# Loading the later image pairs as 32x32 blocks and turning them on VectorE instead of TensorE

## Chip, cores and metric

One NeuronCore of a Trainium2 chip. The metric is device time in microseconds (us) of one execution, the median of several runs. All data is 32-bit float.

## The reference

`x` has 32 images of 14 x 14 tokens with 512 channels. Two layers, each with a group norm (32 groups of 16 channels, over a whole image) in front and a residual around it:

```python
x = x + _L0_conv_ref(_gn(x), block_w, block_b, fc1_w, fc1_b, fc2_w, fc2_b, gammas)
x = x + _L1_conv_ref(_gn(x), W)

# layer 0: 18 blocks, one after the other
for i in range(18):
    nx = gelu(einsum('bhwc,cd->bhwd', x, block_w[i]) + block_b[i])
    if i in (11, 14, 17):
        gates = softmax over 3 anchors of fc2(gelu(fc1(mean of nx over the tokens)))
        nx = nx + gamma[t] * sum of gates * anchors
    x = nx
    if i in (1, 4, 9): anchors.append(x)

# layer 1: a 3x3 convolution, 'SAME', 32 groups of 16 channels
```

## The kernel before, in words

**Tiles.** Activations lie with channels on the 128 partitions and tokens along the row. A tile of work `t` holds two images (N = 392 tokens), a pair `p` two tiles (four images); there are 8 pairs, 0 to 7. The 512 channels are four chunks `c` of 128, two to a "quarter" tile of 128 x 784 (`quarter`, L84).

**A step** is one block (of 18) for one pair: 144 steps. It is done as seven half-size matrix products (a Strassen form; `block`, L371), each of 8 TensorE records (`product`, L387, the matmul is L390). Their PSUM accumulators are X, Y and Z. ScalarE copies them out (`save`, L423), VectorE adds (`add`, L427: c from X, Y or Z), ScalarE applies gelu (L403, or L410 where the token mean is needed), VectorE makes the differences for the next step (`pre_adds`, L369). X is accumulated three times in one bank: after the third product a copy of it is taken, after the fifth an `add` reads it, and the seventh product adds to it again.

**Order of the work.** Everything else is placed between products by hand. A step has seven ticks, one after each product; `calendar` holds what is emitted in a tick, and `put` (L124) looks for the first tick whose budget (`ROOM`, L111; us of VectorE and ScalarE per tick) has room for the cost that the caller names. Each engine works in order, and so does SyncE (SP), which issues nearly all DMAs: a DMA that waits holds up those behind it. The order of steps interleaves two pairs: q's first steps stand among p's last, then q goes on alone with its blocks 6 to 11, and so on.

**The weights** of a step are loaded by `load_block` (L328) in tick 0 of the step before. The four weight sums s0 to s3 of a block are computed once, for pair 0, and kept in DRAM (`skeep`); later pairs load them (`sums`, L346) in ticks 2 to 5 of the step before, each into the one buffer that its product has just set free.

**A pair's start** (`plan_start`, L295): t0 is the first tick of its first step, LEAD is 35 ticks. For each tile, four pieces of 98 tokens x 512 channels are loaded by SP (`load_in`, L245; tag "xin", three buffers), three of them in tick t0 - LEAD - 6, and turned (`turn_in`, L248): four TensorE transposes (L258, tile `tpi`), two copies by ScalarE (L263) that also change the token order within an image from row-major to column-major. The turned tile is written to DRAM (`xkeep`, L271), as the residual needs it at the end. Then the norm's statistics (`stats_in`, L196), scales, and the norm itself in place (L284). Pair 0 is loaded and turned before the first step by the same two functions.

**A pair's end.** After block 17, `gate_base` (L570) on VectorE starts the routed sum, POOL issues four DMAs that add `xkeep` to it in place (`residual`, L666), and `gate_part` (L580), `gate_last` (L594) and `gate_add` (L602) finish it. Layer 1 follows in batches of two pairs: statistics, columns written to DRAM (`x2d`, L699, in pieces of 224 B), reloaded (L817), the convolution as matmuls with band matrices (L838), a sum (L848), a turn back (L862) and the store. The steps between block 17 of pair p and the first step of pair p + 2 are the six steps of pair p + 1 with blocks 6 to 11; so the tick t0 - LEAD - 8 of a pair p + 2 is the last tick of block 17 of pair p.

Of the kernel before, what the change touches and what calls it, by code (L numbers as in the profile page):

```python
# [9 lines left out]
F32 = mybir.dt.float32  # L10
# [9 lines left out]
def kernel(  # L20
# [20 lines left out]
    nc = tc.nc  # L41
    P = 128
    B, H, W, C = x.shape
    HW = H * W
    NCK = C // P
    NH = NCK // 2
    NI = 2
    N = NI * HW
    NT = B // NI
    NPAIR = NT // 2  # L50
    NB4 = 2 * NI
    TS = 4
# [3 lines left out]
    NTG, _, HID = fc1_w.shape  # L56
# [14 lines left out]
    fpool = ctx.enter_context(tc.tile_pool(name="fpool", bufs=1))  # L71
    qpool = ctx.enter_context(tc.tile_pool(name="qpool", bufs=38))
    tmp = ctx.enter_context(tc.tile_pool(name="tmp", bufs=6))
    inpool = ctx.enter_context(tc.tile_pool(name="inpool", bufs=3))
    outpool = ctx.enter_context(tc.tile_pool(name="outpool", bufs=2))
    cvpool = ctx.enter_context(tc.tile_pool(name="cvpool", bufs=2))
    small = ctx.enter_context(tc.tile_pool(name="small", bufs=2))
# [6 lines left out]
    def quarter(name):  # L84
        return qpool.tile([P, NH, N], F32, tag="q", name=name)
# [8 lines left out]
    for p in range(NPAIR - 1):  # L94
        q = p + 1
        if q < NPAIR - 1:
            parts = [(q, 0, 3), (p, 12, 15), (q, 3, 6), (p, 15, 18), (q, 6, 12)]
        else:
            parts = [
                (q, 0, 6), (p, 12, 15), (q, 6, 12), (p, 15, 17), (q, 12, 15), (p, 17, 18),  # L100
                (q, GAP, 0), (q, 15, 18),
            ]
# [12 lines left out]
    def at(tick, fn, *args):  # L115
        calendar[tick].append((fn, args))

    def room(e, tick):
        return left[e].get(tick, ROOM[e][tick % NP7] if tick < tend else TAIL[e])
# [4 lines left out]
    def put(first, need, fn, *args):  # L124

        tick = first
        while any(room(e, tick) < us for e, us in need.items()):
            tick += 1
        for e, us in need.items():
            left[e][tick] = room(e, tick) - us  # L130
        at(tick, fn, *args)
        return tick
# [53 lines left out]
    def stats_tiles(name):  # L186
        d = {"name": name}
        for v, shape in (
            ("st", [NR, 6]), ("mr", [3, NR]), ("dv", [NR, 2]), ("ve", [NR]), ("y", [NR]), ("e", [NR]),
        ):  # L190
            d[v] = small.tile([P] + shape, F32, tag=v, name=f"{v}_{name}")
        return d
# [15 lines left out]
    def scales_mean(d, lo=0, hi=NR):  # L208
        st, mean, dv = d["st"][:, lo:hi], d["mr"][:, 0, lo:hi], d["dv"][:, lo:hi]
        ps = group_sums(f"mps_{d['name']}_{lo}", st[:, :, 1::3], hi - lo)  # L210
        nc.vector.tensor_scalar(mean, ps, 0.5, None, ALU.mult)
        nc.vector.tensor_tensor(
            dv, st[:, :, 1::3], mean.unsqueeze(2).to_broadcast([P, hi - lo, 2]), ALU.subtract
        )
        nc.vector.tensor_mul(dv, dv, dv)
        nc.vector.scalar_tensor_tensor(dv, dv, HW / 2.0, st[:, :, 2::3], ALU.mult, ALU.add)

    def scales_rstd(d, lo=0, hi=NR):

        ps = group_sums(f"vps_{d['name']}_{lo}", d["dv"][:, lo:hi], hi - lo)  # L220
        ve = d["ve"][:, lo:hi]
        nc.vector.tensor_scalar(ve, ps, 1.0 / HW, 1e-5, ALU.mult, ALU.add)
        nc.gpsimd.tensor_tensor(d["y"][:, lo:hi], ve, mhalf[:, lo:hi], ALU.pow)

    def scales_newton(d, lo=0, hi=NR):
        ve, y, e, mr = d["ve"][:, lo:hi], d["y"][:, lo:hi], d["e"][:, lo:hi], d["mr"]
        nc.vector.tensor_mul(e, y, y)
        nc.vector.tensor_mul(e, e, ve)
        nc.vector.tensor_scalar(e, e, -0.5, 1.5, ALU.mult, ALU.add)
        nc.vector.tensor_mul(mr[:, 1, lo:hi], y, e)  # L230
        nc.vector.scalar_tensor_tensor(
            mr[:, 2, lo:hi], mr[:, 0, lo:hi], -1.0, mr[:, 1, lo:hi], ALU.mult, ALU.mult
        )


    xkeep = [
        tc.dram_tile([2, P, NH * N], F32, name=f"xkeep{t}") for t in range(NT)
    ]
    starts = {}
    pst = {}  # L240
# [54 lines left out]
    def plan_start(p):  # L295

        t0 = NP7 * at_step[p, 0]
        parts = [(2 * p + n, s) for n in range(2) for s in range(TS)]
        NIN = 3
        a = t0 - LEAD  # L300
        turned = []
        for j, (t, s) in enumerate(parts):
            at(t0 - LEAD - 6 if j < NIN else turned[j - NIN], load_in, t, s)
            turned.append(put(max(a, turned[j - NIN] + 4 if j >= NIN else 0), {"act": 0.6}, turn_in, t, s))
            a = turned[j] + 1
        b = 0
        for n in range(2):
            for c in range(NCK):
                b = max(b, put(
                    turned[n * TS + TS - 1] + 1, {"dve": 1.0}, stats_in, 2 * p + n, c  # L310
                ))
        b = put(b + 1, {"dve": 0.8}, lambda: scales_mean(pst[p]))
        b = put(b + 1, {"dve": 0.2}, lambda: scales_rstd(pst[p]))
        b = put(b + 2, {"dve": 0.8}, lambda: scales_newton(pst[p]))
        e = b
        for c in range(NCK):
            e = max(e, put(b, {"dve": 1.6}, norm_in, p, c))
        b = e

        assert b < t0  # L320
        at(t0 - 1, take_start, p)
# [290 lines left out]
    def plan_head(p, i):  # L612

        k = at_step[p, i]
        t1 = NP7 * (k + 1)
        name = f"{p}_{i}"
        ti = TARGETS.index(i)
        box = boxes[p, i] = {}
        end = k == len(steps) - 1
        if p == 0:  # L620
            at(t1 + 1, gate_differences, k, ti)
        at(t1 + (0 if end else 1), gate_hidden, k, ti, name, box)
        box["base"] = {
            (h, n): put(t1, {"dve": 1.0}, gate_base, p, i, h, n) for h in range(2) for n in range(2)
        }
        a = t1 + (1 if end else 2)
        while room("dve", a) < 2.2:
            a += 1
        at(a, gate_logits, k, name, box)
        return put(a, {"dve": 2.2}, gate_softmax, ti, name, box)  # L630

    def plan_gates(p, t, a, chunks):

        box = boxes[p, t]
        last = max(a, *box["base"].values())
        for cs in chunks:
            for n in range(2):
                b = a + 1
                adds = []
                for c in cs:  # L640
                    b = put(b, {"act": 0.75}, gate_last, p, t, box, cs, c, n)
                    for i in range(NI):
                        last = max(last, put(a, {"dve": 0.43}, gate_part, p, box, c, n, i))
                    adds.append((c, b + 1))
                for c, b in adds:
                    last = max(last, put(b, {"dve": 0.5}, gate_add, box, cs, c, n))
        return last
# [312 lines left out]
    LEAD = 35  # L960
    for k in range(len(steps)):
        p, i = steps[k]
# [26 lines left out]
    for p in range(NPAIR):  # L989
        plan_differences(p)  # L990
        for i in TARGETS[:-1]:
            a = plan_gates(p, i, plan_head(p, i), [[0, 1], [2, 3]])
# [5 lines left out]
    for p in range(1, NPAIR):  # L998
        plan_start(p)
    ended = {p: plan_end(p) for p in [*range(NPAIR - 2), NPAIR - 1, NPAIR - 2]}  # L1000
    b = NP7
    for g in range(C // CG):
# [3 lines left out]
        for dx in range(3):  # L1006
            b = put(b, {"dve": 1.15 if dx else 0.6}, build_band, g, dx)
# [39 lines left out]
```

## Time and profile before

| what | value |
|---|---|
| median of 3 runs | 2988.8 us (2988.3 to 2991.35) |
| the profiled execution: its time / its span | 2990.1 us / 2988.3 us |
| granted TensorE clock | 0.994 |
| busy: PE / DVE / ACT / POOL | 99% / 58% / 49% / 3% |
| turn, PE records: L258 | 256 matmuls (64 turns of four transposes), 34.4 us busy |
| turn, ScalarE: L263 | 128 copies, 35.4 us busy |
| DMA queue of SP (q1) | 355,178 packets, 436.85 MB, 46.4% of the 16 engines' span |
| DMA queue of ACT (q10) | 25,792 packets, 13.65 MB, 1.7% |
| DMA queue of POOL (q0) | 4,608 packets, 12.85 MB, 2.5% |
| loads of x by SP | 60 of 196 KB, median issue 412 ns |

How to read it: PE is TensorE's matmuls, PEld its weight loads, DVE is VectorE, ACT ScalarE, POOL GpSimd, SP SyncE. A group line names the line of code, the engine, the operation, output and input tiles and shape, and how often it came; then busy us in total, mean ns of one, and how long its engine sat idle just before, with what ended that. The chain of work that ended last is followed back from the last instruction. A timeline row has start, length, engine, line, operation and count, with the idle time before it in brackets. Packets are the pieces in which DMA engines move data.

### The profile page before, as it was taken

To read this page: it belongs to the slowest core of one execution; us is meant where nothing else is said; L and a number is where in the kernel's file an instruction comes from. 1 tells how busy PE (TensorE), PEld (TensorE's weight loads), DVE (VectorE), ACT (ScalarE), POOL (GpSimd) and SP (SyncE) were. 2 spreads that over 40 slices of the span, in tenths; PEclk is the share of its full clock that TensorE was granted. 3 is DMA by queue.
4 is the path that set the end of the run, shared out by engine and by line. 5 is a ranking of instruction groups with operands and counts; after the bars stand their busy time and mean duration, and the time that the engine had idled before them with its cause. 6 is when DMAs were issued, how large, how long until landed. Compare 5 with 4: busy or idle time off the path is not lost.

```text
span 2988.3 us, 31804 instructions
## 1 busy us (share of the span) xinstructions
PE 2945.5 (99%) x10113; PEld 1812.9 (61%) x10113; DVE 1734.0 (58%) x3309; ACT 1457.6 (49%) x3467; POOL 77.8 (3%) x60
## 2 busy tenths in 40 slices
PE   8999999999999999999999999999999999999986
PEld 5555555555566566666666666666666665656666
DVE  6877786655467454673546635565455653545663
ACT  4445445545455444554545544445445554544551
POOL 0000000000000000000000000000000000000010
PEclk9999999999999999999999999999999999999997
DMA  4444436633365345553455544555445653343678
GB/s 159 154 165 139 162 125 191 178 115 116 126 195 156 129 142 162 185 159 132 146 164 174 173 133 133 173 166 173 139 132 168 173 161 121 124 135 118 206 220 210
DMA packets 385743, 465.36 MB, mean 156 GB/s; under 512 B 150715, under 2 KB 213290, under 8 KB 385578
## 3 DMA queue, kind: packets, MB, share of 16 engines
q1 hardware_dynamic: 355178, 436.85, 46.4%
q0 software_dynamic: 4608, 12.85, 2.5%
q10 hardware_dynamic: 25792, 13.65, 1.7%
q8 instruction: 81, 1.33, 0.2%
q14 instruction: 84, 0.69, 0.1%
HBM read 381.48 MB, written 81.79 MB: 155 GB/s over the span
## 4 chain that ended last, share of the span: by engine, by line
PE 98%; DMA 1%; DVE 1%; issue 0%; ACT 0%; SPq 0%; DVEq 0%
PE x L390 51%; PE z L390 25%; PE y L390 13%; PE cps L838 5%; PE lps L522 1%; PE tpo L862 1%; PE tpi L258 1%; PE hps L506 1%; DMA tw<-in_L_conv_W_dram 0%; DMA w<-in_L_conv_fc_w_dram 0%; PE warm L950 0%; DMA w<-in_L_conv_block_w_dram 0%; DMA x2d<-xc 0%; PE mps_b L203 0%; DMA x<-x2d 0%
## 5 line engine op out<-in xcount | busy, mean ns | idle before, releaser
L390 PE MATMUL x<-t,s 128*128 128x392 f32 x2304 | 810.0, 494 | 0.0
L403 ACT ACTIVATE o<-c,bias 128x392 f32<-128x392 f32 x720 | 440.7, 620 | 663.0 <-DVE c L427 658.3
L390 PEld LDWEIGHTS x<-t,s 128*128 128x128 f32 x2304 | 432.5, 190 | 297.5
L427 DVE TENSOR_TENSOR c<-x,c 128x392 f32<-128x392 f32 x288 | 160.8, 565 | 515.5 <-PE x L390 423.8
L423 ACT COPY c<-x 128x392 f32<-128x392 f32 x576 | 278.4, 483 | 352.6 <-PE x L390 347.7
L390 PE MATMUL x<-t,w 128*128 128x392 f32 x1152 | 403.1, 493 | 0.9 <-DVE c L427 0.9
L390 PE MATMUL z<-t,s 128*128 128x392 f32 x1152 | 403.1, 493 | 0.0
L390 PE MATMUL z<-o,s 128*128 128x392 f32 x1088 | 380.9, 493 | 0.0
L390 PE MATMUL y<-o,w 128*128 128x392 f32 x1088 | 380.5, 492 | 0.0
L390 PE MATMUL x<-o,w 128*128 128x392 f32 x1088 | 380.3, 492 | 0.0
L427 DVE TENSOR_TENSOR c<-y,c 128x392 f32<-128x392 f32 x288 | 162.9, 566 | 294.3 <-PE y L390 206.7
L390 PEld LDWEIGHTS x<-t,w 128*128 128x128 f32 x1152 | 217.8, 190 | 157.9 <-DVE c L427 1.5
L390 PEld LDWEIGHTS z<-t,s 128*128 128x128 f32 x1152 | 217.0, 190 | 152.2
L369 DVE TENSOR_TENSOR t<-o,o 128x784 f32<-128x784 f32 x272 | 264.1, 971 | 65.4 <-ACT o L403 63.5
L390 PEld LDWEIGHTS x<-o,w 128*128 128x128 f32 x1088 | 206.4, 190 | 147.2
L390 PEld LDWEIGHTS y<-o,w 128*128 128x128 f32 x1088 | 205.1, 190 | 145.6
L390 PEld LDWEIGHTS z<-o,s 128*128 128x128 f32 x1088 | 205.0, 190 | 145.3
L369 DVE TENSOR_TENSOR t<-o,t 128x784 f32<-128x784 f32 x272 | 264.2, 971 | 4.7
L423 ACT COPY c<-z 128x392 f32<-128x392 f32 x288 | 139.2, 483 | 206.3 <-PE z L390 206.2
L427 DVE TENSOR_TENSOR c<-z,c 128x392 f32<-128x392 f32 x288 | 159.1, 563 | 118.8 <-PE z L390 118.0
L410 ACT ACTIVATE o<-c,bias 128x196 f32<-128x196 f32 x288 | 129.4, 450 | 91.0 <-DVE c L427 90.2
L403 ACT ACTIVATE o<-x,bias 128x392 f32<-128x392 f32 x240 | 137.5, 582 | 72.8 <-PE x L390 67.0
(107 smaller groups left out, 2061.2 us busy)
## 6 DMA issues: line engine op xcount, KB each, us to landing
w<-in_L_conv_block_w_dram SPq DMA_DIRECT2D x144, 1024.0 KB
s<-skeep SPq DMA_DIRECT2D x504, 256.0 KB
x2d<-xc SPq DMA_DIRECT2D x128, 224.0 KB
x<-x2d SPq DMA_DIRECT2D x64, 448.0 KB
skeep<-s SPq DMA_DIRECT2D x72, 256.0 KB
bw<-band SPq DMA_DIRECT2D x38, 384.0 KB
xkeep<-xt SPq DMA_DIRECT2D x32, 392.0 KB
o<-xkeep POOLq DMA_DIRECT2D x32, 392.0 KB, 7.6
```

Source lines behind the costliest of these rows:

```text
L258: nc.tensor.transpose(tp[:, c * TP : (c + 1) * TP], xs[:, c * P : (c + 1) * P], ident[:TP, :TP])
L369: nc.vector.tensor_tensor(t[j], i0, i1, ALU.subtract)
L390: nc.tensor.matmul(acc[d][:, :N], lhsT=lhsT[:, kk, d * P : (d + 1) * P], rhs=rhs[:, kk, :], start=first and kk == 0, stop=kk == NH - 1, sk ...
L403: nc.scalar.activation(o[:, d, :], srcs[d], AF.Gelu_apprx_tanh, bias=bias[:, r : r + 1])
L410: nc.scalar.activation(o[:, d, sl], srcs[d][:, sl], AF.Gelu_apprx_tanh, bias=bias[:, r : r + 1], accum_out=pooled[:, c, m : m + 1],)
L423: nc.scalar.copy(cs[d], acc[d][:, :N])
L427: nc.vector.tensor_tensor(cs[d], acc[d][:, :N], cs[d], ALU.add)
L506: nc.tensor.matmul(hps[:, :NB4], lhsT=w1[:, kk, :], rhs=box["pooled"][:, kk, :], start=(kk == 0), stop=(kk == NCK - 1),)
L522: nc.tensor.matmul(lps[:, m * NB4 : (m + 1) * NB4], lhsT=w2[:, m * P : (m + 1) * P], rhs=h, start=True, stop=True,)
L838: nc.tensor.matmul(pv[:, :, lo:hi], lhsT=d["bw"][:, g, dy], rhs=xv[:, :, lo + dy - 1 : hi + dy - 1], start=j == 0, stop=j == 2, skip_group ...
L862: nc.tensor.transpose(tp[:NV, j * P : (j + 1) * P], d["xs"][:, g, 0, v * NV : (v + 1) * NV], ident)
```

## The change

Only pairs 1 to 7 are touched. (1) `copy_in` copies the four images of a pair from x to a DRAM tensor `xcol[p]` whose tokens stand in column-major order within an image, 30 ticks before t0 - LEAD. (2) `load_blocks` loads one chunk of 128 channels of one tile as blocks: partition q*32+j holds, for channel group q of 32 and token j of each block of 32 tokens, 32 channels; that is 12 blocks of 32 tokens, in pieces of 32 channels (128 B), by four DMAs. Since 392 is not a multiple of 32, the last 32 tokens of all four chunks are loaded once more for each tile (`xr`, four DMAs). (3) `turn_blocks` turns the blocks with one VectorE transpose of 128 x 384, and with every second chunk one of 128 x 64 for the last tokens. (4) The plan charges VectorE instead of ScalarE for a turn, loads the first four chunks in tick t0 - LEAD - 8, lets several turns stand in one tick, and puts a chunk's statistics after its half tile. The pool of loaded pieces has four buffers instead of three. `stats_in`, the norm, `xkeep` and all that follows stay.

```diff
-    inpool = ctx.enter_context(tc.tile_pool(name="inpool", bufs=3))
+    inpool = ctx.enter_context(tc.tile_pool(name="inpool", bufs=4))
...
+    TB = 32
+    NTB = N // TB
+
+    xcol = [None] + [tc.dram_tile([NB4 * HW, C], F32, name=f"xcol{p}") for p in range(1, NPAIR)]
+
+    def copy_in(p):
+        for b in range(NB4):
+            nc.sync.dma_start(
+                xcol[p][b * HW : (b + 1) * HW].rearrange("(w h) c -> w h c", w=W),
+                x[p * NB4 + b].rearrange("h w c -> w h c"),
+            )
+
+    def load_blocks(t, c):
+        d = starts.setdefault(t, {"xin": {}})
+        cols = xcol[t // 2][t % 2 * N : (t % 2 + 1) * N].rearrange("n (k q i) -> q n k i", k=NCK, i=TB)
+        xs = d["xin"][c] = inpool.tile([P, NTB, TB], F32, tag="xin", name=f"xb_{t}_{c}")
+        for q in range(P // TB):
+            nc.sync.dma_start(
+                xs[q * TB : (q + 1) * TB],
+                cols[q, : NTB * TB, c].rearrange("(n j) i -> j n i", j=TB),
+            )
+        if c == 0:
+            xr = d["xr"] = inpool.tile([P, NCK, TB], F32, tag="xr", name=f"xr_{t}", bufs=2)
+            for q in range(P // TB):
+                nc.sync.dma_start(xr[q * TB : (q + 1) * TB], cols[q, N - TB :])
+
+    def turn_blocks(t, c):
+        d = starts[t]
+        if c == 0:
+            d["xq"] = [quarter(f"xt_{t}_{h}") for h in range(2)]
+            if t % 2 == 0:
+                pst[t // 2] = stats_tiles(f"a{t // 2}")
+        xs = d["xin"].pop(c)
+        h, cc = divmod(c, NH)
+        xq = d["xq"][h]
+        nc.vector.transpose(xq[:, cc, : NTB * TB], xs.rearrange("p n i -> p (n i)"))
+        if cc == NH - 1:
+            nc.vector.transpose(xq[:, :, N - TB :], d["xr"][:, h * NH : (h + 1) * NH])
+            nc.sync.dma_start(xkeep[t][h], xq.rearrange("p c n -> p (c n)"))
...
-        parts = [(2 * p + n, s) for n in range(2) for s in range(TS)]
-        NIN = 3
+        parts = [(2 * p + n, c) for n in range(2) for c in range(NCK)]
+        NIN = 4
         a = t0 - LEAD
+        at(a - 30, copy_in, p)
         turned = []
-        for j, (t, s) in enumerate(parts):
-            at(t0 - LEAD - 6 if j < NIN else turned[j - NIN], load_in, t, s)
-            turned.append(put(max(a, turned[j - NIN] + 4 if j >= NIN else 0), {"act": 0.6}, turn_in, t, s))
-            a = turned[j] + 1
         b = 0
-        for n in range(2):
-            for c in range(NCK):
-                b = max(b, put(
-                    turned[n * TS + TS - 1] + 1, {"dve": 1.0}, stats_in, 2 * p + n, c
-                ))
+        for j, (t, c) in enumerate(parts):
+            at(t0 - LEAD - 8 if j < NIN else turned[j - NIN], load_blocks, t, c)
+            turned.append(put(max(a, turned[j - NIN] + 5 if j >= NIN else 0), {"dve": 0.45 + c % NH * 0.15}, turn_blocks, t, c))
+            a = turned[j]
+        for j, (t, c) in enumerate(parts):
+            b = max(b, put(turned[j // NH * NH + NH - 1], {"dve": 0.7}, stats_in, t, c))
```

## The prediction

> **What bounds the kernel now.** I read the page first: the slices of TensorE (PE) and the chain of work that ended last.
>
> ```profile
> PE   8999999999999999999999999999999999999986
> ...
> PE 98%; DMA 1%; DVE 1%; issue 0%; ACT 0%; SPq 0%; DVEq 0%
> ```
>
> PE is full in all but the first and the last slices, and 98% of the chain is PE. In the list of waits no PE instruction of the steady part waits over 1 us in total (0.9 us for a VectorE add is the largest; the 10 us waits for x2d lie in the tail). So time taken off PE comes off the end, one for one, until something else makes PE wait. Next I read the timeline of PE alone where a later pair is turned (columns: start, us, engine, line, operation, tiles, count).
>
> ```profile
> 500.98 2.80 PE L390 MATMUL x<-t,s 128*128 128x392 f32 x8
> 503.61 2.80 PE L390 MATMUL z<-t,s 128*128 128x392 f32 x8
> 506.24 0.50 PE L258 MATMUL tpi<-ident,xin 98*128 98x98 f32 x4
> 506.58 2.82 PE L390 MATMUL x<-t,s 128*128 128x392 f32 x8
> 509.24 0.50 PE L258 MATMUL tpi<-ident,xin 98*128 98x98 f32 x4
> ```
>
> A product starts 2.63 us after the one before it (500.98 to 503.61). With a turn between them the starts lie 3.00 us apart (506.24 to 509.24): the turn takes 0.34 us to the next product, and that product then takes 2.66 instead of 2.63. **One turn_in costs PE 0.37 us**, with its weight loads. I checked the starts of the other pairs' turns: 0.34 us each, back to back with products.
>
> Then the groups by shape (busy us, mean ns of one, idle before):
>
> ```profile
> L787 DVE TENSOR_TENSOR bt<-tw,mask 128x384 f32<-128x384 f32 x96 | 51.3, 553 | 8.2 <-DMA tw<-in_L_conv_W_dram 7.4
> L263 ACT COPY xt<-tpi 128x196 f32<-128x196 f32 x128 | 35.4, 334 | 2.6 <-PE tpi L258 2.2
> ```
>
> Last the DMA side: a window in which x2d is stored in pieces of 224 B, the engines' table around the start of pair 3 (last three columns: clock, DMA share, GB/s), and the residual adds and their first user on VectorE.
>
> ```profile
> DMA packets 4512, 1.57 MB, mean 197 GB/s; under 512 B 4192, under 2 KB 4192, under 8 KB 4512
> ...
> q1 hardware_dynamic: 4512, 1.57, 86.9%
> ```
>
> ```profile
> 810.00:820.00 10.00, 10.00 (x32) 5.83 (x31) 4.94 (x8) 6.38 (x25) 0.00 (x0) 1.00 0.56 177
> 820.00:830.00 10.00, 10.00 (x37) 6.10 (x37) 5.89 (x9) 4.09 (x10) 3.50 (x4) 1.00 0.92 230
> 830.00:840.00 10.00, 10.00 (x43) 6.52 (x42) 6.22 (x19) 4.16 (x11) 0.00 (x0) 1.00 0.87 203
> 840.00:850.00 10.00, 10.00 (x32) 5.83 (x31) 9.24 (x19) 7.40 (x19) 0.00 (x0) 1.00 0.36 127
> ```
>
> ```profile
> 822.51 0.91 POOL L666 DMA_DIRECT2D o<-xkeep  x1 [266.07 <-PE x L390]
> 826.82 2.66 POOL L666 DMA_DIRECT2D o<-xkeep  x3 [3.40 <-PE x L390]
> ```
>
> ```profile
> 835.19 0.76 DVE L580 SCALAR_TENSOR_TENSOR o<-o,g,o 128x196 f32<-128x196 f32 x2
> 835.86 1.03 DVE L427 TENSOR_TENSOR c<-x,c 128x392 f32<-128x392 f32 x2
> 836.81 1.08 DVE L580 SCALAR_TENSOR_TENSOR o<-o,g,o 128x196 f32<-128x196 f32 x3
> ```
>
> The reader is to see that the DMA engines have little room from 820 to 840, just where the first block loads of a pair will be queued, and that VectorE uses the second residual (issued at 826.8, landing a median of 7.2 us and at most 9.9 us later in this stretch) at about 837.4: some 2 us of margin.
>
> [...]
>
> **The change, part by part.**
>
> PE, removed: 7 pairs x 8 turns = 56 turns x 0.37 = **20.7 us**, all on the path. Pair 0 keeps its turns.
>
> ScalarE, removed: 112 of the 128 copies, 35.4 x 112/128 = 31.0 us. It is off the path (ACT 49% busy): worth nothing directly.
>
> VectorE, added per pair: 8 turns of 128x384 and 4 of 128x64 for the last tokens. No row shows the operation. The nearest, the 128x384 L787, takes 553 ns; [...] I take 0.56 us, and 0.22 us for the small ones: 8 x 0.56 + 4 x 0.22 = 5.4 us a pair, 38 us in all (VectorE 58 to 59%). Behind each turn in VectorE's order stand the adds of L427, which free PE's accumulators. X is read by such an add after the fifth product and written again in the seventh: one product, 2.63 us, less two adds of 0.57, leaves 1.5 us for late work. The plan charges a pair 8 x 0.525 = 4.2 us against my 5.4, so at most three ticks are overbooked by some 0.4 us each, under the 1.5. VectorE has 2 to 5 us idle in every 10 from 850 to 880. Cost at 0.56 us: nothing. Without that cover it would be those 1.2 us a pair, 8 us. The 0.7 us stats and the norms keep their count and move by ticks, with five steps (about 95 us) to the pair's first step.
>
> SP and DMA, per pair: 44 issues in place of 8 loads (4 copies, 32 block loads, 8 for the last tokens); xkeep stays. Block packets are 128 B: 8 x 1536 + 2 x 512 = 13,312 a pair. The price of one is not shown. In the x2d window 0.869 x 16 x 8 us = 111 us went to 4512 packets: 24.6 ns each is an upper value for 224 B, since 320 of them are 2 KB; scaled by bytes (1.57 MB in 111 us, 14.1 B/ns) 128 B would be 9.1 ns. A dearer end is the ACT queue, mostly 512 B: 1.7% x 16 x 2988 / 25,792 = 31.5 ns. I take **16 ns**, range 9 to 31.5. In all 93,000 packets, 93 us of the 16 engines' time: 51% share becomes 54%. The copy in DRAM moves as many 2 KB rows as the old loads did, but writes them to DRAM; it is issued 22 ticks (58 us) ahead of its readers and holds up only loads with a step, 18.4 us, of time.
>
> The burst counts. In tick t0-43, the last of a step, 20 DMAs are issued at once: 4 blocks and the first rest, 4 x 1536 + 512 = 6656 packets, 0.416 us for each ns of a packet: 6.7 us at 16 ns. On SP they take 20 x 0.41 = 8.2 us (median issue of the old loads), so the next step's weight load, issued at 819.35 in this pair, slips by about 5.5 us. It is needed at the next step's start, near 838, and takes some 5 us: 8 us are left. The s loads have a step each. Room for the burst from 816.7 to 835: 1.5 + 0.8 + 0.7 = 3.0 us by the shares above, plus 2.4 us of the three old loads that are gone from there (0.6 MB at 250 GB/s). So 6.7 - 5.4 = 1.3 us of lateness meets the 2 us margin of the second residual. Nothing is lost at 16 ns. Loads of blocks 5 to 8 have five ticks, 13 us, for 1.5 us of data each.
>
> Sum: 2990.1 (the profiled execution; span 2988.3 and 1.8 around it) - 20.7 + 0.9 (one more wait of the size the trace has once, for a tick that I misjudge) = 2970.3. The median of the runs is 1.3 below that execution: **2969.0 us**.
>
> **Rivals.**
> 1. VectorE's turn is dear: [...] Half a us to 2 us in two ticks of 7 pairs, about 10 us: **2979**. For: four turns may share one tick, and pair 1 falls where VectorE is 80% busy. Against: the gaps above.
> 2. **Slower**: the burst makes the residual late. VectorE waits in L580, the adds and pre-additions queue behind it, PE stops. It begins when the burst passes 5.4 + 2 + 1.5 = 8.9 us, 21.4 ns a packet, in the 6 pairs that have a pair ending there (2 to 7). The gain is eaten at 8.9 + 20.7/6 = 12.35 us, **29.7 ns a packet**. [...] For: DMA at 0.92 there, landing margins of 2 us. Against: pieces of 224 B cost under 24.6 ns.
> 3. No difference: burst near 27 ns, or both small losses together: **2988**.
>
> **How the numbers follow.** Forecast 0.68 (own range 2966 to 2975), rival 1 0.12, rival 2 0.14, rival 3 0.06. A measurement tells about 0.2%, 6 us, from no change: faster means below 2982.8. Faster 0.68 and nearly all of rival 1, 0.79; within 0.07; slower 0.14. The range takes the forecast and rival 1 and leaves out the other two: 2966 to 2983; the low end is 2 us of turns that cost more than 0.37.
>
> **What would show it.** L258 x32 matmuls in place of 256 records; starts of products 2.63 us apart around each pair's start; the turn group on VectorE near 560 ns; packets of 128 B near 16 ns; L580 and L427 without waits for DMA; POOL's landing near 7 to 10 us. Wrong if PE shows gaps at L390 released by c of L427, or w or s by DMA, near 480, 835, 1192, 1560, 1923 and 2291.

## The result

The changed kernel takes 2968.9 us (median of 4 runs, 2967.3 to 2972.0); the kernel before took 2989.9 beside it (2988.3 to 2991.4). The ratio is 0.9931, 95% interval 0.9914 to 0.9948. The prediction said 2969.0. Its profiled execution took 2968.65 us with a span of 2966.6.

The page of the changed kernel: the slices of PE, the chain, and SP's DMA queue (packets, MB, share of the 16 engines).

```profile
PE   8999999999999999999999999999999999999996
...
q1 hardware_dynamic: 452450, 448.79, 49.4%
...
PE 96%; DVE 1%; DMA 1%; SPq 1%; issue 0%; ACT 0%; DVEq 0%
```

PE still sets the end. In its timeline where pair 3 is turned, these products start 2.63 us apart, where the old one had 3.00 at each turn.

```profile
851.30 2.80 PE L431 MATMUL x<-t,w 128*128 128x392 f32 x8
853.93 2.80 PE L431 MATMUL x<-o,w 128*128 128x392 f32 x8
856.56 2.80 PE L431 MATMUL y<-o,w 128*128 128x392 f32 x8
859.20 2.80 PE L431 MATMUL x<-t,s 128*128 128x392 f32 x8
```

The operations by line (ns: least, median, most; then first and last start), VectorE's turns and what is left of ScalarE's copies:

```profile
L274 DVE STREAM_TRANSPOSE xt<-xb x56: 534/572/579, 158.8 to 2321.5; 128x384 f32<-128x384 f32 x56
L276 DVE STREAM_TRANSPOSE xt<-xr x28: 245/245/247, 159.9 to 2322.1; 128x64 f32<-128x64 f32 x28
...
L306 ACT COPY xt<-tpi x16: 337/339/343, 5.1 to 11.0; 128x196 f32<-128x196 f32 x16
```

**Where the 21.7 us of span went.** The first product of the first step starts at 21.87 us before and at 22.31 after, the last at 2879.27 and 2860.25. From first to last product that is 2857.4 against 2837.9: **19.5 us** from the part that the change touches. The tail after the last product shrank from 109.0 to 106.4 us, and the head grew by 0.4. The tail is not the change's doing: in copy_only below, whose tail is the code of before, it took 105.2.

The stretch of the burst at pair 3. First the engines' table (last three columns: clock, DMA share, GB/s), then SP's timeline:

```profile
807.00:817.00 10.00, 10.00 (x31) 5.71 (x31) 6.71 (x9) 6.40 (x26) 0.00 (x0) 1.00 0.63 180
817.00:827.00 10.00, 10.00 (x45) 6.64 (x43) 4.11 (x7) 3.82 (x8) 3.49 (x4) 1.00 0.89 144
827.00:837.00 10.00, 10.00 (x35) 6.10 (x36) 7.96 (x21) 5.45 (x13) 0.00 (x0) 1.00 1.07 293
837.00:847.00 10.00, 10.00 (x31) 5.71 (x31) 9.12 (x21) 7.02 (x18) 0.00 (x0) 1.00 0.38 129
```

```profile
812.31 1.96 SPq L256 DMA_DIRECT2D xb<-xcol  x4
814.32 2.55 SPq L263 DMA_DIRECT2D xr<-xcol  x4
816.91 7.92 SPq L256 DMA_DIRECT2D xb<-xcol  x12
824.94 0.55 SPq L369 DMA_DIRECT2D w<-in_L_conv_block_w_dram  x1
825.59 7.78 SPq L387 DMA_DIRECT2D s<-skeep  x4
835.69 0.38 SPq L369 DMA_DIRECT2D w<-in_L_conv_block_w_dram  x1
```

The 20 DMAs of the burst kept SP for 12.6 us, 0.63 us each, and the weight load behind them was issued at 824.94, 10.4 us later than its tick. It also took longer to land. By its semaphore it landed at 835.13, 10.2 us after its issue and 0.4 us ahead of the step that uses it; in the kernel before it landed 5.8 us after its issue, with 15.1 us to spare. The DMA queues between 824.9 and 830.7, from its issue to the first packet of its size (packets, MB, share of the 16 engines):

```profile
q0 software_dynamic: 360, 1.00, 95.6%
q1 hardware_dynamic: 714, 0.09, 13.4%
```

q0 is POOL's queue, which carries the residual adds: their packets, 2.8 KB in the mean, had nearly all of the engines' time, and SP's queue (q1) still had small pieces of the burst to move. So the late weight load ran into the residual adds. In pairs 2 to 7, where a pair ends beside the burst, it landed 9.0 to 12.3 us after its issue (5.6 to 6.1 before); in pair 1, where none does, 5.8. The residual adds in the same stretch, and their users on VectorE:

```profile
817.73 0.91 POOL L707 DMA_DIRECT2D o<-xkeep  x1 [260.63 <-PE x L431]
822.03 2.68 POOL L707 DMA_DIRECT2D o<-xkeep  x3 [3.39 <-PE x L431]
...
DMA to landing us min/median/max: 5.2/6.2/8.6
```

```profile
830.41 0.76 DVE L621 SCALAR_TENSOR_TENSOR o<-o,g,o 128x196 f32<-128x196 f32 x2
832.03 1.08 DVE L621 SCALAR_TENSOR_TENSOR o<-o,g,o 128x196 f32<-128x196 f32 x3
```

No wait stands before either row: the residual landed in time, and here no later than before (5.8/7.2/9.9). The list of waits has something else that is new. On VectorE, in the turn of pair 1 (us in total, times, longest):

```profile
DVE s L395 <- DMA w<-in_L_conv_block_w_dram: 3.3, 1, 3.3
```

and in the timeline of PE's weight loads, at pairs 4 and 6:

```profile
1190.13 2.46 PEld L431 LDWEIGHTS x<-o,w 128*128 128x128 f32 x8 [0.17 <-DMA w<-in_L_conv_block_w_dram]
...
1915.62 2.27 PEld L431 LDWEIGHTS x<-o,w 128*128 128x128 f32 x8 [0.52 <-DMA w<-in_L_conv_block_w_dram]
```

So the weights of the next step came just at its start. They cost PE nothing in pair 4 and 0.2 us in pair 6, since PE's weight loads for a product start some 0.33 us ahead of its matmuls (1187.46 and 1187.79 for the product before, in pair 4), but the 8 us that the prediction left them were gone.

### The profile page after: what moved, and what is told of

It reads as the page before. It is cut to its first block, busy times and chain, and to the rows that moved or that the text cites. A ratio compares the mean times of both kernels' runs of the same rounds, so it can differ in the third digit from the quotient of the medians.

```text
span 2966.6 us, 31628 instructions
## 1 busy us (share of the span) xinstructions
PE 2926.8 (99%) x9889; PEld 1795.7 (61%) x9889; DVE 1764.8 (59%) x3393; ACT 1430.9 (48%) x3355; POOL 78.1 (3%) x60
## 3 DMA queue, kind: packets, MB, share of 16 engines
q1 hardware_dynamic: 452450, 448.79, 49.4%
## 4 chain that ended last, share of the span: by engine, by line
PE 96%; DVE 1%; DMA 1%; SPq 1%; issue 0%; ACT 0%; DVEq 0%
PE x L431 50%; PE z L431 25%; PE y L431 13%; PE cps L879 5%; PE lps L563 1%; PE tpo L903 1%; PE hps L547 1%; SPq L740 0%; SPq L256 0%; SPq L851 0%; DMA x<-x2d 0%; PE warm L991 0%; DMA w<-in_L_conv_block_w_dram 0%; DMA xin<-in_x_dram 0%; DMA x2d<-xc 0%
```

## The experiments

**Theory** after this profile: the gain is PE time alone; VectorE's turns are covered; the margin that the burst eats is that of the weight load queued behind it on SP. **Rivals**: part of the gain comes from ScalarE or from work that moved; VectorE is near its limit; the burst's limit is the residual, through the load of the DMA engines.

### pe_back: PE's work put back

```diff
         nc.vector.transpose(xq[:, cc, : NTB * TB], xs.rearrange("p n i -> p (n i)"))
+        tp = aux(f"tpi_{t}_{c}")
+        for j in range(NCK):
+            nc.tensor.transpose(tp[:, j * TP : (j + 1) * TP], ident[:TP, :], ident[:TP, :TP])
```

> The changed kernel with the PE work of the old turns put back: beside each of the 56 VectorE turns stand four TensorE transposes of a constant into an unused accumulator, no copy by ScalarE, nothing else moved. If the gain is PE time alone, at 0.37 us a turn, all of it goes: 2968.9 + 20.5 = about 2989. If part of the gain came from the ScalarE copies that are gone or from the new place of other work, the time stays below 2985.

Measured: 2987.9 us (2986.0 to 2993.5), 0.9991 of the kernel before (0.9980 to 1.0001). From first to last product it took 2856.5 us: of the 19.5 us gained, 18.5 are gone again. The gain was PE time; what ScalarE no longer does, and the new places of other work, are worth at most the 1 us left.

### dve_twice: each VectorE turn done twice

```diff
-        nc.vector.transpose(xq[:, cc, : NTB * TB], xs.rearrange("p n i -> p (n i)"))
+        for _ in range(2):
+            nc.vector.transpose(xq[:, cc, : NTB * TB], xs.rearrange("p n i -> p (n i)"))
```

> The changed kernel with each 128x384 VectorE turn done twice, so that a turn costs about 1.14 us[...]. If VectorE's gaps cover it: within 3 us of the changed kernel, 2969 to 2972, with new PE waits only around pair 1, where VectorE is fullest. If the turns are near the limit (the prediction's first rival): 10 us or more, 2979 to 2985, with PE waiting for c of the adds in every pair.

Measured: 2970.8 us (2966.9 to 2972.4), ratio 0.9934 (0.9918 to 0.9951). The rows by line, then waits:

```profile
L275 DVE STREAM_TRANSPOSE xt<-xb x112: 535/578/580, 159.9 to 2327.9; 128x384 f32<-128x384 f32 x112
...
PE x L432 <- DMA w<-in_L_conv_block_w_dram: 0.9, 2, 0.7
...
PE x L432 <- DVE c L469: 0.7, 1, 0.7
PE x L432 <- ACT c L465: 0.7, 1, 0.7
PE y L432 <- ACT o L445: 0.7, 1, 0.7
```

56 x 0.578 = 32 us more on VectorE made the products' part 3.6 us longer than in the changed kernel (2841.5 us). I expected new waits around pair 1 alone; by the steps' starts 1.3 us of the loss lie there, 2.1 in pair 3 and 0.3 in pair 6, in part as waits for w and s. VectorE's gaps cover nine tenths of a doubled turn; the first rival falls.

### copy_only: the copies in DRAM alone

```diff
         a = t0 - LEAD
+        at(a - 30, copy_in, p)
         turned = []
```

with `copy_in` and `xcol` as in the change, in the kernel before.

> The kernel before with nothing but the copies in DRAM added, 28 of 401 KB that nobody reads. If they are hidden, as the prediction has it: 2989 to 2991, no wait of PE for w or s. If they hold up the weight loads behind them: 5 us or more, 2995 and up, with PE waits 65 ticks ahead of each pair's first step.

Measured: 2990.2 us (2987.8 to 2996.6), ratio 1.0004 (0.9995 to 1.0012). From first to last product 2857.65 against 2857.40: the copies are hidden. No step stands out by as much as 0.3 us. Its tail, on unchanged code, was 3.8 us shorter than in the profile of before (two waits of the tail for DMA alone, for the gates' weights and for x2d, went from 5.5 to 3.5 and from 10.2 to 9.5): such differences between two profiles are not to be read as an effect.

### pile: a heavier burst

```diff
+    def pile_up(p):
+        dum = quarter(f"dum_{p}").rearrange("p c n -> p (c n)")[:112].rearrange("p (k n i) -> p k n i", k=7, n=7)
+        for k in range(7):
+            nc.sync.dma_start(
+                dum[:, k], xcol[p].rearrange("(j n) c -> j n c", n=7)[:, :, k * TB : k * TB + TB // 2]
+            )
...
             at(t0 - LEAD - 8 if j < NIN else turned[j - NIN], load_blocks, t, c)
+            if j == NIN - 1:
+                at(t0 - LEAD - 8, pile_up, p)
```

> The changed kernel with a heavier burst: behind the first block loads of each pair, in the same tick, seven more DMAs load 5488 pieces of 64 B that nobody reads. Theory now: the limit that the burst meets first is the next step's weight load, queued behind it on SP (in the profile of the changed kernel the weight loads of PE wait for it by 0.2 and 0.5 us in two pairs). Then PE waits for w at the start of the step after the burst, 3 to 6 us in each of 7 pairs: 2990 to 3010. The prediction's slower rival says the residual: VectorE waits for it, about 2 us in 6 pairs, 2980. If there is room for both: 2969.

Measured: 3011.8 us (3007.4 to 3016.2), ratio 1.0076 (1.0060 to 1.0091): slower than before. The list of waits:

```profile
PEld x L440 <- DMA w<-in_L_conv_block_w_dram: 35.9, 7, 8.3
PE x L440 <- DMA w<-in_L_conv_block_w_dram: 31.6, 7, 7.7
```

Seven waits of PE for w, one a pair; no engine waits for the residual (landing 4.7/6.4/11.3 us over the run, 4.7/7.4/13.0 in the changed kernel). The weight load is the limit, as the theory had it. It was issued 16 to 22 us after its tick, when the residual adds had landed, and then took 5.7 to 6.6 us; so here all of the delay was SP's. PE's timeline and the engines' table at pair 2 show a second loss:

```profile
508.02 5.51 PE L440 MATMUL x<-o,w 128*128 128x392 f32 x8 [7.71 <-DMA w<-in_L_conv_block_w_dram]
513.36 2.80 PE L440 MATMUL y<-o,w 128*128 128x392 f32 x8
```

```profile
500.00:510.00 10.00, 2.29 (x4) 1.18 (x4) 4.54 (x7) 1.75 (x5) 0.00 (x0) 0.65 0.88 246
510.00:520.00 10.00, 10.00 (x27) 5.54 (x26) 4.30 (x11) 5.10 (x13) 0.00 (x0) 0.83 0.38 143
520.00:530.00 10.00, 10.00 (x32) 5.83 (x31) 7.64 (x16) 6.35 (x15) 0.00 (x0) 1.00 0.41 99
```

After the wait of 7.71 us the next product takes 5.34 us (508.02 to 513.36) instead of 2.63; the granted clock in the two stretches is 0.65 and 0.83. In six of the seven pairs the product after the wait is 1.8 to 2.8 us longer, 15 us in all; with the 31.6 us of waits that is the 47 us by which the products' part grew over the changed kernel.

### tick_later: the burst behind the weight load

```diff
-            at(t0 - LEAD - 8 if j < NIN else turned[j - NIN], load_blocks, t, c)
+            at(t0 - LEAD - 7 if j < NIN else turned[j - NIN], load_blocks, t, c)
```

> The changed kernel with the first block loads one tick later (tick t0 - 42, the first of a step, in which SP issues the next weight load ahead of them). The weight load is out of the burst, and the burst stands full beside the four residual adds. If the weight load is the near limit: PE's weight loads wait for w nowhere, the time is that of the changed kernel or up to 1 us less, 2968 to 2969. If the residual is (the prediction's slower rival): VectorE waits for it in 6 pairs, 2972 or more.

Measured: 2966.1 us (2963.1 to 2967.1), ratio 0.9921 (0.9907 to 0.9934). No wait for w is left on PE, its weight loads or VectorE; the residual lands 4.9/6.7/10.7 us after its issue and nobody waits for it. The interval overlaps that of the changed kernel (0.9914 to 0.9948), so the times don't tell the two apart. By the timelines the products' part is 2836.9 us, 1.1 shorter, but 1.3 of that is a wait in step 2, long ahead of any block load, which the profiles of the next two experiments lack as well. Pairs 1 and 6 have back what they lost in the changed kernel, 0.7 us. Pair 3's start loses 1.2 us, where it lost 0.3 in the changed kernel: PE waits for s loads there (0.4 us at 878.55). They stand on SP behind the later block loads, which kept it for 12.8 us.

### pile_after_w: the heavier burst behind the weight load

As pile, with both `LEAD - 8` changed to `LEAD - 7`.

> The same tick, and the seven unread loads behind the first block loads. Theory (SP's order decides): no PE wait for w; SP is busy for some 25 us from the step's start, so the s loads behind the burst come 3 to 5 us late for the third product of the next step, 20 to 35 us in all with the slower clock after each wait: 2985 to 3005, PE waiting for s. The residual's rival: VectorE waits for the residual ahead of all that. If only the DMA engines' load counted, and not SP's order, there would be no wait for s, about 2969.

Measured: 2968.0 us (2965.7 to 2971.3), ratio 0.9927 (0.9913 to 0.9941). The same 27 DMAs that cost 43 us in pile cost nothing that these times show one tick later. SP's timeline at pair 3:

```profile
819.55 11.42 SPq L256 DMA_DIRECT2D xb<-xcol  x12
831.08 4.70 SPq L268 DMA_DIRECT2D dum<-xcol  x7
835.88 2.00 SPq L396 DMA_DIRECT2D s<-skeep  x4
837.97 0.38 SPq L378 DMA_DIRECT2D w<-in_L_conv_block_w_dram  x1
```

No wait for w, as expected. Of the late s loads that I expected, almost nothing came: SP was done with the burst 22.6 us after the step's start, not 25, and at pair 3 the four s loads, issued from 835.9 on, were in time. In pair 2 they were not quite. The third product of the next step starts 0.7 us late at 497.8, and the s load that it waits for landed 0.1 us before; the list of waits names VectorE and ScalarE, but what they did at that moment this product does not use. The step is 0.9 us longer, a step in pair 6 0.3, and the 20 to 35 us stayed away. The residual stood in the middle of this burst and landed in 4.8/6.7/10.6 us: at this load, the rival that loads the DMA engines until the residual is late falls. What decides is which load stands behind the burst in SP's order. The load of the engines has a part in how long SP is held: the seven unread loads took SP 4.7 us here, behind the residual adds, and 9.8 in pile, beside them.

### later_bands: room on VectorE at pair 1

```diff
-    b = NP7
+    b = NP7 * 11
     for g in range(C // CG):
```

on top of tick_later.

> As tick_later, and the band matrices of layer 1 are built from step 11 on instead of step 1, so that VectorE has room where pair 1 is turned. The traces give pair 1 a gain of 2.3 us where pairs 2 to 7 have 2.9: if VectorE's fullness is the cause, pair 1 has 2.9 too and the steady part is 0.6 us shorter than in tick_later, 2967.5 to 2968.5, too little for the times to tell. If the bands are late for their first use or press on another stage, PE waits there: 2972 or more.

Measured: 2966.3 us (2963.7 to 2968.1), ratio 0.9919 (0.9907 to 0.9932), as tick_later. Compared at the steps' starts, pair 1's turn gains 2.9 us here (2.4 in the changed kernel, where I had read 2.3), but it gains 2.9 in tick_later already, with the bands where they were. So my reading, that VectorE was too full there, falls. The 3.3 us wait in the list above is the cause that fits: in pair 0 the weight sums are made on VectorE from w itself, the burst held w up, the sums waited, and what stood behind them came late to PE. tick_later has neither the wait nor the loss. In this trace pair 3's wait for s is absent too: every pair gains 2.9 us, and the products' part is 2835.7.

## Why the prediction was right, and where its steps were not

- **PE, 20.7 us removed**: right. Pairs 2, 4, 5 and 7 gain 2.9 us each, 0.367 us a turn. Pairs 1, 3 and 6 gain 2.4, 2.6 and 2.8, by late w and s loads; the whole of the products' part gains 19.5. pe_back shows that PE's time is the cause.
- **VectorE's turn at 0.56 and 0.22 us**: measured 0.572 and 0.245. The 0.56 stood on the 553 ns of L787; no trace of before showed the 0.22, nor a turn as dear as rival 1 made it. Covered: of the time that dve_twice added, only a tenth came to PE. The rival at 2979 was 8 us too dear even for a turn at 1.14 us.
- **Packets of 128 B at 16 ns**: the share of q1 went from 46.4% of 16 x 2988.3 us to 49.4% of 16 x 2966.6, 1263 us more for 97,272 more packets: 13.0 ns. The records of the 128 B packets themselves give 13.1 ns. Inside the bounds; the 5.4 us of the burst that it makes did not hold up the residual.
- **SP's 8.2 us for the burst, and 8 us left for the weight load**: this step failed. I priced the new issues with the 412 ns of the old loads; they took 0.63 us each, 12.6 in all, and the weight load slipped by 10.4 us, not 5.5. And I let it land in the 5 us of an unloaded moment; slipped, it met the residual adds and took 9.0 to 12.3 us in pairs 2 to 7. I had set the residual against the burst, and not against the weight load. What was left in pairs 3, 4 and 6 was 0.4 us or less: PE's weight loads waited 0.2 and 0.5 us in two pairs, and pair 1 lost 0.5 us by sums that waited for w. The step of the later block loads, 13 us for 1.5 us of data each, has the same fault: twelve of their issues kept SP for 11.9 us in pair 3, and an s load behind them came 0.3 us late. The range held because these losses stayed that small.
- **The slower rival, by the residual**: wrong in its place. No run shows a wait for the residual, with pile_after_w the hardest test. A burst can make this kernel slower than before (pile, 3012 us), but through the weight load behind it in SP's queue. How much of SP's time there is the issues' own, and how much comes from engines that are busy, the runs don't separate.
- **The sum** came out within 0.2 us partly by luck. The products' part is right on its own: 20.7 less 0.9 for a wait is 19.8, and the small waits did come to about 1 us, though not from a misjudged tick. But the head and the tail made the profiled execution 2.2 us shorter for other reasons, and the median, put 1.3 us below that execution, lay 0.2 above it. These two nearly cancel.

## What to carry to other kernels

Where one engine sets the end, work moved off it is worth the time by which it had pushed its neighbours apart in that engine's timeline: here to within 1% (0.367 us a turn against 0.37), where nothing else waited. VectorE, with two fifths of its time free (58% busy before), took the work over, and nine tenths of it even at twice the price. When a change adds many small DMAs to an in-order issue queue, price the issues themselves: here they took SP 0.63 us each in the burst, where the old loads took 0.41. Ask first which transfer stands behind them, when it is needed, and what other traffic it will meet if it slips; moving the burst to the other side of that transfer was here the whole difference between pile (3011.8 us) and pile_after_w (2968.0).

## What the runs showed of the hardware

- A VectorE transpose of the kernel's 32x32 blocks of 32-bit data, 128 x 384, took 572 ns (median), and 128 x 64 took 245: from the two, an estimate of 1.02 ns an element along the row and some 180 ns fixed.
- SP issued its DMAs in the program's order: at pair 3 of the changed kernel the weight load's issue (824.94) follows directly on the last of the burst (816.91 + 7.92 us), 10.4 us after its tick. SP's longest wait for PE there, 16.3 us at an s load, passed with nothing issued.
- A DMA of 48 KB in pieces of 128 B took SP 468 ns to issue (median), one of 16 KB 597 ns, against 384 for a 1 MB load; in the burst, 0.63 us each. Single issues of the same 48 KB form took from 0.30 to 2.28 us.
- A 1 MB weight load landed 5.6 to 6.1 us after its issue in the kernel before, at the seven steps after a burst's place, and 9.0 to 12.3 us where it met the residual adds of another queue.
- Around PE's waits in pile its granted clock was lower: 0.65 and 0.83 in the two stretches of 10 us from 500 on, at the wait of 7.71 us, and 0.66 from 2325 to 2335, at that of 3.13; it was 1.00 from 1590 to 1600, right after that of 2.48. The products after the waits of 3.13, 3.15, 4.04, 5.11, 5.94 and 7.71 us took 5.4, 4.4, 5.2, 4.9, 5.4 and 5.3 us instead of 2.63; the one after the wait of 2.48 us took 2.74.
